# An attention and gated feed-forward block on one core: other lags, durations and placing times in the planner that writes out TensorE's order

## The chip, the cores and the metric

The kernel runs on one core of a Trainium2 chip. The metric is the device time of one execution in microseconds (us), median of three runs. The engines are named as in the profile: PE is TensorE (matmuls, with PEld for its weight loads), DVE is VectorE, ACT is ScalarE, POOL is GpSimd and SP is SyncE, which issues most of the DMAs. PSUM is the memory into which PE writes; each of its eight banks holds 128 rows of 512 float32 values.

## The reference

Two sequences of 1024 tokens with 512 features are normalised. A causal attention with 32 heads of 16 features and a linear position bias (ALiBi) runs on them, and beside it a gated feed-forward net whose weights are reduced to three values and combined by the octonion table. The result is `x + attention * silu(feed-forward)`.

```python
def block(x):
    xn = layernorm(x)                                  # 2 x 1024 x 512
    q, k, v = split(xn @ w_qkv.T + b_qkv)              # 32 heads of 16
    scores = q @ k.T / 4 + slope[head] * position      # causal: later keys get -1e9
    s = softmax(scores) @ v @ w_out.T + b_out
    gate, up = oct(xn, ternary(w_gate)), oct(xn, ternary(w_up))
    g = silu(oct(silu(gate) * up, ternary(w_down)))
    return x + s * g
```

## The kernel before

Attention is cut into 32 units: (batch, group of four heads, half of the queries). A unit is named here as batch/group/half, so 1/0/1 is batch 1, group 0, second half. A unit of half 0 sees 512 keys, one of half 1 sees 1024; they are called first-half and second-half units below.

A unit is worked through in these steps, and every PE step has a matching step on another engine:

- Maxima. PE multiplies queries and keys (L537) into one of two PSUM banks ("x" banks), DVE adds the causal mask on the diagonal blocks and reduces each row to its maximum (`left`, `mx`). `split_max` splits the maxima into two parts on DVE.
- Placing (`place_max`). PE transposes the maxima (L602, tile `pm`), ACT copies them to `mr`, and POOL issues two small DMAs that write `mr` into two rows of the query tile (`q_stack<-mr`). The next product then subtracts the maximum by itself.
- Exponentials. PE multiplies keys and queries again, with the maxima in them (L653), into one of three banks ("e" banks), adds the causal mask by a bf16 matmul on diagonal blocks (L670), and ACT writes `exp` into the tile `p`. The first of these matmuls in a unit waits for the placing DMAs.
- Values. PE multiplies `p` with the values (L689, tile `po`), four matmuls side by side on different columns of the array. `normalise` copies the sum (ACT), transposes it (PE, L709), divides (DVE) and stores it (SP).

Between these, PE also has "side" work that feeds later units or uses finished ones: the projections of queries and keys (L466, `pqk`) and of values (L424, `pv`), the transposes of tokens and weights (L390, L360) and the output projection (L742, L758). These share two "m" banks with the placing and the normalising. Projected queries and keys go through DRAM (`sp<-st`) and come back by SP's DMAs into rings of four query and five key tiles (`k_stack<-sp`, `q_stack<-sp`).

The order in which all of this is issued is not written as loops. A planner in the kernel's Python code (L1046 to the end of `step`) keeps a model clock `now` for PE, and `act` and `dve` for two other engines, in nanoseconds. In each step it has a list of things that could come next, each with the time `ready` at which its banks and inputs are free by the model and with a rank; it takes one, emits its instructions, and moves the clocks. `step` stays with score products (L537, L653) while one is ready within `SOON = 80` of now, and otherwise takes other work that is ready. `SWITCH` is the model's cost of a change between four kinds of matmul: R (scores), V (values), B (bf16 masks), F (all others). The emitted order of PE, ACT, DVE, POOL and SP is kept as it is during the attention.

The model's numbers are therefore what decides the order, and they cost nothing themselves on the chip. The ones in question:

- an ACT or DVE step starts 150 after its matmul has been issued, and its bank is free again 60 after the step's end;
- an exponential takes 510 on ACT, other PSUM copies on ACT take 500, a normalising 600 on DVE;
- `placed[u]`, the time from which the first exponential product of unit `u` may be issued, is 3500 after the model's free time of the placing bank, which is the end of the ACT copy.

After the attention, the feed-forward net runs in an order of plain loops (L1387 and L1421). Its preparation (the splitting of tokens, the expansion of weights) is not held to that order and is moved up by the scheduler into the last units of the attention.

## Time and profile before

| | us |
|---|---|
| median of three runs | 1151.21 (1150.77 to 1151.92) |
| profiled execution, its own time | 1150.65 |
| span of the profiled execution | 1148.9 |
| start: loads, first norms and projections | 0 to 50.0 |
| units of attention, from the first L537 to the last L689 | 50.0 to 849.1 |
| last output projections, then feed-forward net | 849.1 to 1148.9 |

Over the units' stretch of 799.1 us, PE is busy for 746.3 us, DVE for 592.4, ACT for 402.7 and POOL for 71.9, and the mean granted clock of PE is 0.98. A busy PE is not a PE at its peak: a matmul's end is modelled, and lies some 0.16 us behind the point at which the next one may start. PE's useful work is therefore counted below from the spacing of matmuls that follow each other without a wait.

The wait of an engine is put down to the instruction that released it. Idle time on an engine that does not set the end costs nothing by itself.

### The profile page before, as it was taken

What the parts mean: (1) busy time and instruction counts of PE and PEld (TensorE: products, weight loads), DVE (VectorE), ACT (ScalarE), POOL (GpSimd) and SP (SyncE); (2) the same over time, 40 slices, a digit from 0 to 9 for tenths busy, and PEclk for the clock granted to TensorE, in tenths of its full rate; (3) what the DMA queues carried; (4) which work ended last, traced back from release to release, by engine and by line L of the source; (5) the groups of instructions that cost most, each with busy time, mean ns of one, the idle gap of its engine ahead of it and who ended that gap; (6) DMA issues with size and microseconds to landing.
All of it is one profiled execution on the core that took longest, in us unless ns stands there. A gap on an engine that the chain in (4) does not pass through costs nothing.

```text
span 1148.9 us, 15597 instructions
## 1 busy us (share of the span) xinstructions
PE 1067.9 (93%) x5562; PEld 680.9 (59%) x5562; DVE 679.0 (59%) x1400; ACT 500.9 (44%) x962; POOL 176.8 (15%) x295
## 2 busy tenths in 40 slices
PE   7979979999999999989999999899889999999996
PEld 5644545664555665545565555555446687878784
DVE  5368787667777687767787768777641123141211
ACT  4122656645554544535435444465582122232222
POOL 6401023100011010010110000001001123242322
PEclk9899979999999999989999999999899999999998
DMA  6975563453744608082542542831041013030200
GB/s 194 206 147 142 112 169 85 69 87 90 140 112 88 127 2 158 2 195 38 140 66 52 102 90 85 142 62 52 25 140 68 29 45 110 1 110 1 76 35 37
DMA packets 73740, 104.24 MB, mean 91 GB/s; under 512 B 26992, under 2 KB 31120, under 8 KB 73664
## 3 DMA queue, kind: packets, MB, share of 16 engines
q1 hardware_dynamic: 66336, 87.48, 34.8%
q10 hardware_dynamic: 3552, 9.78, 2.7%
q0 software_dynamic: 3776, 5.98, 2.1%
q8 instruction: 45, 0.74, 0.3%
q14 instruction: 31, 0.25, 0.1%
HBM read 69.58 MB, written 33.10 MB: 89 GB/s over the span
## 4 chain that ended last, share of the span: by engine, by line
PE 67%; DVE 12%; DMA 9%; ACT 5%; issue 5%; POOL 2%; SPq 1%; ACTq 0%; DVEq 0%; POOLq 0%
PE s L537 11%; PE s L653 11%; PE po L689 11%; PE pqk L466 6%; PE pg L1387 6%; PE pu L1387 6%; PE pd L1421 5%; DVE mx L69 5%; PE pout L758 4%; DMA q_stack<-mr 3%; PE pv L424 3%; DVE s L69 2%; PE s L670 2%; DVE left L69 1%; ACT p L69 1%
## 5 line engine op out<-in xcount | busy, mean ns | idle before, releaser
L69 ACT ACTIVATE p<-s 128x512 f32<-128x512 f32 x576 | 302.3, 599 | 222.7 <-PE s L670 142.0
L537 PE MATMUL s<-k_stack,q_stack 126*128 126x512 f32 (+3 forms) x768 | 276.3, 417 | 28.2 <-DVE mx L69 22.4
L653 PE MATMUL s<-q_stack,k_stack 128*128 128x512 f32 (+3 forms) x768 | 221.5, 373 | 17.3 <-DMA q_stack<-mr 12.9
L69 DVE TENSOR_REDUCE mx<-s 128x1 f32<-128x384 f32 (+3 forms) x352 | 226.2, 643 | 11.7
L69 DVE TENSOR_REDUCE left<-s 128x1 f32<-128x512 f32 x256 | 169.0, 686 | 86.2 <-PE s L537 85.2
L537 PEld LDWEIGHTS s<-k_stack,q_stack 126*128 126x128 f32 x768 | 133.1, 193 | 128.6 <-issue 33.3
L653 PEld LDWEIGHTS s<-q_stack,k_stack 128*128 128x128 f32 x768 | 135.2, 192 | 74.4 <-ACT p L69 30.2
L69 DVE TENSOR_TENSOR s<-s,mask 128x128 f32<-128x128 f32 (+2 forms) x352 | 124.2, 353 | 62.2 <-PE s L537 61.1
L689 PE MATMUL po<-p,v 128*32 128x512 f32 (+3 forms) x1536 | 143.0, 491 | 0.1
L466 PE MATMUL pqk<-xnT,wq 128*128 128x512 f32 x256 | 131.3, 614 | 4.5 <-POOL wq L69 2.2
L69 DVE SCALAR_TENSOR_TENSOR h<-pu,sc_u,sg 128x512 f32<-128x512 f32 (+1 forms) x44 | 33.1, 751 | 166.1 <-PE pu L1387 158.7
L69 POOL DMA_DIRECT2D q_stack<-mr x64 | 32.0, 505 | 583.6 <-ACT mr L69 583.6
L689 PEld LDWEIGHTS po<-p,v 128*32 128x32 f32 x1536 | 43.4, 109 | 78.8 <-issue 67.3
L69 POOL TENSOR_TENSOR hs<-h,hs 128x512 fp32r<-128x512 f32 (+1 forms) x44 | 57.6, 1309 | 190.1 <-ACT hs L69 190.1
L69 ACT ACTIVATE sg<-pg,sc_g 128x512 f32<-128x512 f32 (+1 forms) x44 | 30.2, 687 | 100.2 <-PE pg L1387 95.3
L424 PE MATMUL pv<-wv,xnT 128*128 128x256 f32 x256 | 68.2, 383 | 1.5 <-DVE v L69 1.5
L758 PE MATMUL pout<-wo_sb,oT 128*128 128x512 f32 x128 | 61.1, 597 | 2.0 <-ACT oT L69 1.0
L466 PEld LDWEIGHTS pqk<-xnT,wq 128*128 128x128 f32 x256 | 47.1, 198 | 26.6 <-issue 18.1
L69 ACT CAST hs<-h 128x512 fp32r<-128x512 f32 (+1 forms) x44 | 27.3, 620 | 75.3 <-DVE h L69 75.3
L670 PE MATMUL s<-mask,ident 128*128 128x256 bf16 (+1 forms) x320 | 52.0, 257 | 0.0
L424 PEld LDWEIGHTS pv<-wv,xnT 128*128 128x128 f32 x256 | 45.8, 190 | 9.8 <-issue 3.2
L69 ACT CAST mr<-pm 8x512 fp32r<-8x512 f32 x32 | 18.3, 572 | 70.7 <-PE pm L602 67.2
(142 smaller groups left out, 1081.1 us busy)
## 6 DMA issues: line engine op xcount, KB each, us to landing
sp<-st SPq DMA_DIRECT2D x32, 512.0 KB
k_stack<-sp SPq DMA_DIRECT2D x128, 128.0 KB
q_stack<-sp SPq DMA_DIRECT2D x128, 128.0 KB
wqr<-in_wqk_dram ACTq DMA_DIRECT2D x16, 512.0 KB
xt<-in_x_dram SPq DMA_DIRECT2D x16, 256.0 KB
att<-o SPq DMA_DIRECT2D x32, 128.0 KB
ot<-att SPq DMA_DIRECT2D x16, 256.0 KB
proj<-y SPq DMA_DIRECT2D x16, 256.0 KB
```

What stands on the lines that cost most here:

```text
L69: ins = issue(*args, **kwargs)
L424: nc.tensor.matmul(ps[:, 0:256], lhsT=xnT[:, c, b * S + kt * P : b * S + (kt + 1) * P], rhs=wv_tiles[2 * b + hh][:, c, :], start=(c == 0), ...
L466: nc.tensor.matmul(ps, lhsT=wq_tiles[b, gp][:, kt, which, :], rhs=xnT[:, kt, b * S + c * 512 : b * S + (c + 1) * 512], start=(kt == 0), st ...
L537: nc.tensor.matmul(ps[:, j * n : (j + 1) * n], lhsT=q_of(b, g, qc)[0 : NR - 2, first + j, tl * P : (tl + 1) * P], rhs=k_of(b, g, c)[0 : NR ...
L653: nc.tensor.matmul(ps[:, c0 : c0 + w], lhsT=k_of(b, g, kt // 4)[0:NR, h, kt % 4 * P : (kt % 4 + 1) * P], rhs=q[0:NR, h, 512 - w : 512], st ...
L670: pe(nc.tensor.matmul(out, lhsT=ident16, rhs=rhs, start=False, stop=True))
L689: nc.tensor.matmul(po[32 * i : 32 * i + 32, 512 - w : 512], lhsT=v[:, kt, h * VC : h * VC + 32], rhs=p[:, i * part + c0 : i * part + c0 + ...
L758: nc.tensor.matmul(ps, lhsT=turned[t][:, c, :], rhs=wo_sb[0][:, c, :], start=(c == 0), stop=(c == KD - 1),)
L1387: nc.tensor.matmul(ps[:fs, :], lhsT=fw[mt][:, n0 + kt, 0:fs], rhs=part[:, kt, :], start=(kt == 0 and n == 0), stop=(kt == KD - 1 and n == 1),)
L1421: nc.tensor.matmul(pd, lhsT=hs[k][:fs, n, st * P : (st + 1) * P], rhs=fw[mt][:fs, 8:12, :].rearrange("p s n -> p (s n)"), start=(mt == 0 a ...
```

## The change

Only the planner's numbers change. `START` and `END` are new names for the lag before a step of ACT or DVE and the lag behind it. Every instruction stays, in number and in form; what changes is the order in which they are emitted, on each engine.

```diff
     SOON = 80
+    START, END = 210, 160
     RUN = 1800
...
             end = run_dve(
-                now[0] + 150,
+                now[0] + START,
                 heads_in * cost * 1.04 + 70 + (heads_in * 135 + 70) * diagonal,
             )
-            take(x_free)[0] = end + 60
+            take(x_free)[0] = end + END
             if n == count - 1:
                 split_max(*units[u], mtiles[u])
-                turns.append((u, run_dve(end, 500) + 100))
+                turns.append((u, run_dve(end, 500) + END))
...
-            end = run_act(now[0] + 150, 510)
-            e_free[e_free.index(HELD)] = end + 60
+            end = run_act(now[0] + START, 485)
+            e_free[e_free.index(HELD)] = end + END
             if i == (3 if len(pieces) == 1 or pieces[0][3] == 384 else 2):
-                p_ready[cells_at[u] + n] = end + 60
+                p_ready[cells_at[u] + n] = end + END
...
                 place_max(*units[u], mtiles[u])
                 run_pe("F", ready, 436)
-                take(m_free)[0] = run_act(now[0] + 150, 500)
-                placed[u] = m_free[0] + 3500
+                take(m_free)[0] = run_act(now[0] + START, 480) + END
+                placed[u] = m_free[0] + 6000
...
                 normalise(*units[u])
                 run_pe("F", t2, 436)
-                take(m_free)[0] = run_dve(now[0] + 150, 600)
+                take(m_free)[0] = run_dve(now[0] + START, 500) + END
...
             if n == last:
-                o_free[0] = run_act(now[0] + 200, 500)
-                norms.append((u, o_free[0] + 100))
+                o_free[0] = run_act(now[0] + START, 480) + END
+                norms.append((u, o_free[0]))
...
             if what == "v":
-                end = run_dve(now[0] + 150, 350)
+                end = run_dve(now[0] + START, 350)
             elif what == "qk":
-                end = run_dve(run_act(now[0] + 150, 600), 700)
+                end = run_dve(run_act(now[0] + START, 600), 700)
...
             elif what == "t":
-                end = run_act(now[0] + 150, 500)
+                end = run_act(now[0] + START, 480)
             else:
-                end = run_dve(now[0] + 150, 600)
-            m_free[m_free.index(HELD)] = end + 60
+                end = run_dve(now[0] + START, 600)
+            m_free[m_free.index(HELD)] = end + END
...
             if what == "t":
-                take(m_free)[0] = run_act(now[0] + 150, 500)
+                take(m_free)[0] = run_act(now[0] + START, 480) + END
```

## The prediction

> **What bounds the kernel now.** I read the page, then the waits, then each unit's stretch (from its first exponential product, L653, to the next unit's).

> The slices show PE nearly full everywhere and DVE at seven tenths until the feed-forward net; ACT has room. The waits say what PE's gaps end on.

> ```profile
> PE   7979979999999999989999999899889999999996
> DVE  5368787667777687767787768777641123141211
> ACT  4122656645554544535435444465582122232222
> ```

> ```profile
> PE s L537 <- DVE mx L69: 22.4, 55, 3.3
> PE s L653 <- DMA q_stack<-mr: 12.9, 7, 3.6
> PE s L653 <- ACT p L69: 3.4, 6, 1.3
> ```

> Two waits lead: maxima that wait for DVE to free an x bank (55 times), and first exponentials that wait for the placing DMA (7 times, up to 3.6 us). PEld loses another 10.6 us to the same DMA. The timeline of PE before unit 1/0/1 shows the worst:

> ```profile
> 498.16 0.60 PE L602 MATMUL pm<-ident,rm 128*8 128x128 f32 x4
> ...
> 503.13 0.41 PE L537 MATMUL s<-k_stack,q_stack 126*128 126x384 f32 x1 [0.24 <-DVE mx L69]
> 507.11 1.62 PE L653 MATMUL s<-q_stack,k_stack 128*128 128x512 f32 x3 [3.56 <-DMA q_stack<-mr]
> ```

> The transposes of the maxima end at 498.6, the DMA lands at 507.0, and PE had 4.2 us of work for these 8.4 us. The third view gives the engines' busy time by stretch (PE, PEld, DVE, ACT, POOL, then the granted clock):

> ```profile
> 342.70:366.70 24.00, 21.89 (x127) 13.14 (x126) 19.80 (x44) 8.91 (x16) 3.05 (x3) 1.00 0.30 73
> 366.70:389.00 22.30, 22.09 (x141) 13.06 (x142) 14.48 (x30) 14.36 (x28) 1.00 (x2) 1.00 0.75 144
> 389.00:410.70 21.70, 20.91 (x132) 15.03 (x130) 18.66 (x44) 6.63 (x13) 2.92 (x10) 1.00 0.46 69
> 722.00:743.70 21.70, 18.84 (x112) 11.29 (x111) 18.86 (x43) 7.71 (x15) 1.00 (x2) 1.00 0.96 164
> ```

> Rows one, three and four are first-half units: DVE works 18.7 to 19.8 us of 21.7 to 24.0, most of it on maxima of later units. The second row, a second-half unit, gives it only 14.5 of 22.3. So PE bounds the attention on average, and in first-half stretches DVE stands just behind it.

> **PE's work.** From spacing without waits: 0.43 us per pass of a 512-wide float32 matmul (two passes each), 0.43 for a 256-wide one in both passes, 0.11 for a transpose, 0.24 for a 512-wide score, 0.06 to 0.11 for a mask, 1.8 for eight 512-wide value matmuls in two rounds of four. Summed over either order this is 648.7 us before and 649.1 after, of the 799.4 us that the stretches take. Some 150 us are waits, changes of kind and slow clock; only these can move.

> **Part 1, `placed` at 6000.** For each unit I summed PE's work between its L602 and its first L653 in both orders, and set the measured time from L602 to the DMA's landing against it. Work before, work after, landing, in us: 0/0/0 3.96, 7.26, 8.17; 0/1/1 2.19, 3.22, 3.62; 0/2/1 3.77, 6.44, 5.82; 0/3/1 4.24, 7.46, 5.24; 0/4/1 3.38, 6.81, 4.55; 0/5/1 4.25, 6.63, 6.42; 1/0/1 4.24, 7.46, 8.38; 1/1/1 4.25, 6.63, 6.58; 1/5/1 3.83, 6.20, 6.62; 1/7/1 1.24, 4.92, 3.45; and the one that gets worse, 1/6/1, 4.16, 2.60, 4.09. Everywhere else the work is longer than the landing. The shortfall, landing less work where positive, is 23.5 us before and 4.1 after: 19.4 us less.

> **What is late next: DVE.** The work moved ahead of those first exponentials is to a good part maxima, and it moves into first-half stretches. I priced DVE's maxima from its rows (0.61 us a step for `left`, 0.85 to 1.38 for mask and `mx` by shape) and took the change in each stretch to its measured busy time. In 342.7:366.7 PE's work goes from 19.3 to 21.0 us and DVE's from 19.8 to 23.5; in 480.3:507.1 PE's from 19.3 to 23.4 and DVE's from 19.5 to 23.0; in 768.1:786.4 PE's from 15.5 to 16.7 and DVE's from 15.1 to 19.6.

> Each of the 33 stretches is then the longer of two sums: PE's work + 2.7 us + its shortfall, or DVE's busy time + an idle rest. The 2.7 is what stretches without a shortfall show over their work (21.7 for 19.0, 24.5 for 21.9, 25.5 for 22.8). DVE's idle rest has no row of its own, as DVE alone binds hardly anywhere now: it is at most the 2.8 us of 722.0:743.7, the least seen, and at least nothing. With 2.8 the sum over all stretches falls by 1.1 us, with nothing by 12.3, with 2.2 by 5.1 (774.4 to 769.3). I take 2.2, nearer the row. So the 19.4 us shrink to **-5.1**, with -12.3 and -1.1 as ends.

> **Part 2, lags 210 and 160, exps 485.** The new lags put 0.86 us between an e bank's matmul and its next use; the trace shows 0.21 from issue to an idle ACT's start, 0.60 for the exp and 0.05 to the next matmul, the same 0.86. Nearest reuse: banks used again with less work between than they need are short by 14.3 us in sum before and 14.1 after for e, 36.7 and 33.9 for x: -3.0. Longer chains get denser: over five tiles in a row the shortfall grows from 12.8 to 19.4 (e) and from 63.5 to 73.2 (x); these windows overlap fourfold, so +4.1. I take the middle, **+0.6**, with -3.0 and +4.1 as ends.

> **Part 3, changes of kind.** PE changes between R, F, V and B 767 times in the old order and 827 in the new; R to F and back grow by 27 each. The stretch 457.0:480.3 has 3.0 us over its work for some 24 changes, so one costs at most 0.125 us: 60 cost 0 to 7.5. About half lie under waits for banks or DVE: **+3.6**.

> **Part 4, the clock.**

> ```profile
> 78.60:82.00 3.40, 3.35 (x10) 2.48 (x11) 1.38 (x2) 0.71 (x2) 0.00 (x0) 0.50 0.04 11
> 505.30:512.10 6.80, 4.99 (x10) 3.32 (x11) 1.01 (x3) 2.83 (x5) 0.00 (x0) 0.50 0.88 180
> 812.50:822.70 10.20, 8.49 (x24) 5.90 (x24) 9.08 (x23) 3.34 (x6) 1.00 (x2) 0.50 0.06 16
> ```

> The clock is granted at 0.50 in five spells; two of them follow PE's waits of 3.3 and 3.8 us for the placing DMA (0/0/0 and 1/0/1). Half of the time in which PE ran in them is lost: 3.4/2 + 5.0/2 = 4.2 us. In the new order these waits fall to 0.9 us each, so **-4.2** (ends -4.2 and 0). The spell at 812.5 follows a DVE step of the feed-forward preparation and stays.

> [...]

> Nothing moves in the feed-forward net, which follows the last unit. POOL and SP issue the same DMAs in nearly the same order, and their landings are taken as they were.

> **Sum.** 1150.65 (own time of the profiled execution, 1.75 over its span) -5.1 +0.6 +3.6 -4.2 = 1145.6. The median lies 0.6 over the profiled execution, so I forecast **1146**. Its own range is 1138 (DVE's rest near nothing) to 1148.8.

> **Rivals.** Only a difference of over 0.2%, 2.3 us, can be told from no change here.

> *Given back, no change (0.18).* DVE's rest is 2.8, one spell stays: -1.1 +0.6 +3.6 -2.5 = +0.6, so 1152. For it: DVE is at 86% in row three already, where the placing never waited. Against: x banks are reused less tightly.

> *DVE takes the place of the placing, slower (0.36).* PE issues the moved maxima in a bunch into two x banks, waits for DVE inside first-half stretches, and exponentials find less other work between them in the second-half ones. With 3.0 us of rest Part 1 gains nothing, with 4.0 it costs 4.2; then +4.2 +0.6 +3.6 and no clock gained is +8.4, so 1160. It decides from a rest of 3.0. For it: in six first-half stretches (0/2/0 to 0/5/0, 1/0/0, 1/1/0) DVE now rests over 4 us. Against: in most of these PE waits for the placing meanwhile.

> *The placing lands later too (0.06 of the 0.36).* The late landings (over 5 us) fall together with the fills of key and query tiles. If these meet the DMA again and the shortfall stays at 23.5, the stretches' sum grows by 6.3 instead: +10.5 with the two other parts, 1162. Against: the work is 6.2 to 7.5 us, and most landings took 3.3 to 4.

> **Chances and range.** Faster 0.46, within 0.2% 0.18, slower 0.36. The ends reach from all gains (-12.3, -3.0, 0, -4.2: 1131) to 1162; 1135 to 1160 leaves one in ten on each side.

> **What would show it.** Right: PE's waits on `q_stack<-mr` fall from 12.9 to under 4 us, and no half clock at 78 and 505. DVE is at over 90% in the stretches of 0/5/0, 1/0/0 and 1/6/0, and `mx` waits grow. Wrong: waits on the placing as long as before, or PE's waits on `mx` above 35 us, or first-half stretches longer by over 2 us each without shorter second-half ones.

## The result, and the profile after

The changed kernel takes 1158.25 us (median of five runs, 1155.54 to 1159.65) against 1151.92 (1150.77 to 1152.98) for the kernel before: a ratio of 1.0054, 95% interval 1.0038 to 1.007. It is slower by half a per cent, where 1146 was forecast. The profiled execution is the fastest of the five: 1155.54, span 1153.8, 4.9 over that of the kernel before. The attention's units take 802.9 us of it (50.4 to 853.3) against 799.1; start and end add 0.4 and 0.7.

The slices of the page and PE's waits after (line and tile, the releaser; us in total, times, longest):

```profile
PE   7889979999999999699999999899889999999996
DVE  4386786767768677577787777778642123141211
ACT  4122646654653543436436455364682122232321
PEclk9899979999999999799999999998899999999998
```

```profile
PE s L537 <- DVE mx L69: 31.1, 37, 11.4
PE s L653 <- ACT p L69: 8.0, 10, 1.6
PE s L653 <- DMA q_stack<-mr: 0.4, 1, 0.4
```

The wait for the placing is gone, 12.9 us to 0.4, as the change meant it. The maxima wait fewer times (37 for 55) but longer, and one of these waits alone is 11.4 us. It lies in the one dent of PE's row (slice 17), where the granted clock dips too. PE's timeline there, at the first exponentials of unit 0/7/1:

```profile
460.45 0.70 PE L653 MATMUL s<-q_stack,k_stack 128*128 128x512 f32 x2 [0.45 <-DMA q_stack<-mr]
472.61 0.77 PE L537 MATMUL s<-k_stack,q_stack 126*128 126x512 f32 x1 [11.45 <-DVE mx L69]
```

Two exponentials are issued, then nothing for 11.45 us. DVE is named, but DVE was itself waiting for ACT:

```profile
470.91 0.75 DVE L69 SCALAR_TENSOR_TENSOR st<-pqk,bqk_sb,st 128x512 fp32r<-128x512 f32 x1 [11.46 <-ACT st L69]
```

ACT's timeline (ACTq is its instruction that starts a DMA):

```profile
448.11 0.69 ACT L69 ACTIVATE st<-pqk,bqk_sb 128x512 fp32r<-128x512 f32 x1 [0.17 <-PE pqk L466]
...
455.18 0.69 ACT L69 ACTIVATE st<-pqk,bqk_sb 128x512 fp32r<-128x512 f32 x1 [0.29 <-PE pqk L466]
455.32 0.82 ACTq L69 DMA_DIRECT2D wqr<-in_wqk_dram  x2
470.19 0.69 ACT L69 ACTIVATE st<-pqk,bqk_sb 128x512 fp32r<-128x512 f32 x1 [14.32 <-DMA sp<-st]
```

ACT stands for 14.3 us before writing a third projected tile. `st` has two buffers, so the third has to wait until the first, written at 448.1, has been stored (`sp<-st`). Why that store was late stands in SP's timeline:

```profile
434.47 1.71 SPq L69 DMA_DIRECT2D q_stack<-sp  x4
459.25 2.17 SPq L69 DMA_DIRECT2D k_stack<-sp  x4
461.47 0.28 SPq L69 DMA_DIRECT2D k_stack<-al_dram  x1
461.85 0.39 SPq L69 DMA_DIRECT2D att<-o  x1
462.33 1.84 SPq L69 DMA_DIRECT2D q_stack<-sp  x4
464.39 0.38 SPq L69 DMA_DIRECT2D sp<-st  x1
```

SP issues nothing from 436 to 459, and the store comes fifth behind a fill of a key tile for unit 1/0. What the fill waited for is in the waits of SP:

```profile
SPq L69 <- DMA wqr<-in_wqk_dram: 34.9, 4, 23.1
```

That is a load of projection weights. The fill neither reads nor overwrites them. What links the two stands in the DMAs' records in the traces: in both kernels SP's and ACT's DMAs signal on the same eight semaphores, 101 and 104 to 110. The load issued at 455.32 signals on 101, last at 459.24; the first DMA of the fill waits for 101 and is issued at 459.25.

```
ACT   455.32  wqr <- weights in DRAM         signals on 101
SP    459.25  key fill <- sp, first of four  waits for 101, signals on 101
```

So SP stands until a load has landed that ACT issues only at 455.32. It is a chain of four steps between two engines: ACT issues the weights late; SP's fill waits for them; the store behind the fill is late; ACT needs that store's buffer. ACT keeps its emitted order, so the exponentials stand behind that `st` (the next comes at 470.8), DVE's half of `st` too, then the x banks, then PE.

The stretch of 0/7/1 shows the price (PE, PEld, DVE, ACT, POOL busy, granted clock, DMA share, GB/s); first before, then after:

```profile
457.00:480.30 23.30, 22.96 (x133) 12.60 (x132) 16.61 (x32) 14.12 (x27) 1.00 (x2) 1.00 0.08 26
```

```profile
345.50:370.00 24.50, 23.80 (x137) 15.66 (x134) 20.55 (x48) 7.76 (x14) 1.03 (x2) 1.00 0.68 141
460.50:493.90 33.40, 21.46 (x126) 12.17 (x127) 16.28 (x32) 14.21 (x27) 2.92 (x10) 0.80 0.52 119
493.90:519.60 25.70, 25.07 (x133) 13.89 (x131) 21.17 (x47) 9.46 (x17) 0.99 (x2) 1.00 0.59 114
770.60:794.90 24.30, 21.63 (x120) 12.54 (x119) 19.91 (x42) 7.94 (x15) 2.88 (x3) 0.90 0.27 56
```

Unit 0/7/1 takes 33.4 us where it took 23.3, and PE's work in it, counted as in the prediction, is 17.5 where it was 20.3: 12.9 us are lost in this one stretch, more than the units lost in all (3.8). All other units together are then faster than before.

The other rows are the three first-half stretches in which DVE was forecast at over 90%. It is at 84% (20.55 of 24.50), 82% and 82%. Only the last, 1/6/0, got longer as feared: 24.3 us for 18.3. There PE issues nothing but maxima from 786 to 795, in step with DVE.

The clock, in the stretches at half speed that are new:

```profile
281.20:284.70 3.50, 3.50 (x17) 1.62 (x19) 2.04 (x3) 3.50 (x7) 0.08 (x1) 0.51 0.59 238
462.10:475.80 13.70, 3.19 (x8) 2.38 (x9) 4.43 (x10) 3.34 (x6) 0.00 (x0) 0.50 0.91 226
745.50:748.90 3.40, 3.40 (x9) 2.53 (x10) 0.99 (x2) 2.02 (x4) 0.00 (x0) 0.50 0.40 140
789.80:800.10 10.30, 9.29 (x21) 6.43 (x22) 8.63 (x18) 3.78 (x7) 0.00 (x0) 0.50 0.00 0
```

The spells at 78 and 505 went, as forecast, but these came, and one of 3.4 us at 90: 54.6 us at half clock in the units for 34.1. Two of them lie in the jam and in the run of maxima of 1/6/0. (The columns are those of the stretches.)

### The profile page after: what moved, and what is told of

Read it like the earlier page. It is cut to its first block, busy times and chain, and to the rows that moved or that the text cites. A ratio compares the mean times of both kernels' runs of the same rounds, so it can differ in the third digit from the quotient of the medians.

```text
span 1153.8 us, 15593 instructions
## 1 busy us (share of the span) xinstructions
PE 1069.0 (93%) x5562; PEld 682.2 (59%) x5562; DVE 677.9 (59%) x1400; ACT 500.8 (43%) x962; POOL 177.0 (15%) x295
## 3 DMA queue, kind: packets, MB, share of 16 engines
q1 hardware_dynamic: 66336, 87.48, 34.5%
## 4 chain that ended last, share of the span: by engine, by line
PE 72%; DVE 12%; issue 5%; DMA 5%; ACT 4%; POOL 2%; SPq 0%; ACTq 0%; DVEq 0%; POOLq 0%
PE s L537 12%; PE s L653 12%; PE po L689 11%; PE pqk L466 7%; PE pg L1388 6%; PE pu L1388 6%; PE pd L1422 5%; DVE mx L69 5%; PE pout L758 4%; PE pv L424 3%; DVE s L69 2%; PE s L670 2%; PE pm L602 1%; DMA ot<-att 1%; ACT p L69 1%
## 5 line engine op out<-in xcount | busy, mean ns | idle before, releaser
L69 ACT ACTIVATE p<-s 128x512 f32<-128x512 f32 x576 | 303.3, 600 | 184.4 <-PE s L670 125.0
L537 PE MATMUL s<-k_stack,q_stack 126*128 126x512 f32 (+3 forms) x768 | 278.4, 421 | 38.0 <-DVE mx L69 31.1
L653 PE MATMUL s<-q_stack,k_stack 128*128 128x512 f32 (+3 forms) x768 | 225.3, 379 | 8.6 <-ACT p L69 8.0
L69 DVE TENSOR_REDUCE mx<-s 128x1 f32<-128x384 f32 (+3 forms) x352 | 226.3, 643 | 11.8
L537 PEld LDWEIGHTS s<-k_stack,q_stack 126*128 126x128 f32 x768 | 133.7, 195 | 149.7 <-issue 51.7
L69 DVE TENSOR_REDUCE left<-s 128x1 f32<-128x512 f32 x256 | 168.7, 685 | 83.2 <-PE s L537 81.8
L653 PEld LDWEIGHTS s<-q_stack,k_stack 128*128 128x128 f32 x768 | 136.0, 194 | 60.4 <-ACT p L69 26.2
L69 DVE TENSOR_TENSOR s<-s,mask 128x128 f32<-128x128 f32 (+2 forms) x352 | 124.1, 353 | 60.8 <-PE s L537 59.7
L69 DVE SCALAR_TENSOR_TENSOR h<-pu,sc_u,sg 128x512 f32<-128x512 f32 (+1 forms) x44 | 33.0, 751 | 166.3 <-PE pu L1388 158.7
L69 POOL DMA_DIRECT2D q_stack<-mr x64 | 32.4, 511 | 622.2 <-ACT mr L69 622.2
L69 POOL TENSOR_TENSOR hs<-h,hs 128x512 fp32r<-128x512 f32 (+1 forms) x44 | 57.5, 1307 | 190.2 <-ACT hs L69 190.2
L69 ACT ACTIVATE sg<-pg,sc_g 128x512 f32<-128x512 f32 (+1 forms) x44 | 30.2, 687 | 100.9 <-PE pg L1388 95.5
L69 ACT ACTIVATE st<-pqk,bqk_sb 128x512 fp32r<-128x512 f32 x32 | 22.0, 689 | 113.6 <-PE pqk L466 71.8
L69 ACT CAST hs<-h 128x512 fp32r<-128x512 f32 (+1 forms) x44 | 27.3, 620 | 75.2 <-DVE h L69 75.2
```

Source lines behind the costliest of these rows:

```text
L69: ins = issue(*args, **kwargs)
L537: nc.tensor.matmul(ps[:, j * n : (j + 1) * n], lhsT=q_of(b, g, qc)[0 : NR - 2, first + j, tl * P : (tl + 1) * P], rhs=k_of(b, g, c)[0 : NR ...
L653: nc.tensor.matmul(ps[:, c0 : c0 + w], lhsT=k_of(b, g, kt // 4)[0:NR, h, kt % 4 * P : (kt % 4 + 1) * P], rhs=q[0:NR, h, 512 - w : 512], st ...
```

## Experiments

Two theories at first. *The link*: the loss is the jam in 0/7/1, and comes from a store and a fill behind a late load on another engine's queue. *The order*: the new order is worse by itself (DVE in the place of the placing, changes of kind), and the jam is one of its faces. Two edits cut the link in different places, and each was also made to the kernel before as control. In the diffs, `act_`, `sp_` and `pool_` are the engines that issue.

**Loads of wqr issued by POOL.** ACT then issues only the first of these loads, at the start, and the orders of PE, DVE and SP stay as they are. In the changed kernel, and in the kernel before:

```diff
-                load_wq((n // NP, n % NP), act_)
+                load_wq((n // NP, n % NP), pool_)
```

> The changed kernel with one edit: the loads of the query and key weights (wqr) are issued by POOL and not by ACT; the orders of PE, DVE and SP stay as they are. Theory (a jam on SP's queue): in the changed kernel the fill of a key tile stands on SP behind a completion count that it shares with a wqr load, which ACT issues only at 455.3; the store of a projection (sp<-st) stands behind that fill, ACT's next st waits 14.3 us for the store, and PE idles 11.4 us and then runs at half clock. With the load off ACT the fill no longer waits for it: the wait of ACT st on sp<-st goes, the stretch 460 to 494 falls from 33.4 us to 20 to 22, and the kernel takes 1143 to 1148 us. Rival (VectorE has taken the place of the placing): the jam is hidden behind DVE's work or returns elsewhere; 1154 to 1159 us.

> The kernel before with the same edit, as a control. Theory: the old order has no projection store that anybody waits for behind such a fill (ACT never waits for sp<-st there), so the edit is worth little: 1147 to 1153 us; a part of the late placings may go if they came from fills that start late. Rival (the edit itself is what gains, in any order): it falls by as much as in the changed kernel, 8 us or more.

Measured: the changed kernel 1143.89 us, ratio to before 0.9932 [0.9908, 0.9956]; the control 1145.29, 0.9945 [0.9926, 0.9963]. In the first, SP waits for no wqr any more, ACT waits for no `sp<-st`, and 0/7/1 takes 22.7 us. The jam is gone, and the changed kernel has lost its handicap. But the kernel before gains as well, more than its bounds allowed, which was worth learning; with this edit the two kernels can't be told apart. Some of its late placings had the same root: 1/0/0 shrinks from 26.8 to 22.5 us, and half of PE's wait on the placing goes (12.9 before), as its waits show:

```profile
PE s L537 <- DVE mx L69: 24.3, 61, 3.5
PE s L653 <- DMA q_stack<-mr: 6.8, 4, 3.4
```

**The store `sp<-st` issued by POOL.** The link between the load and the fill stays; the store no longer stands behind the fill. The orders of PE, DVE and ACT stay.

```diff
-            sp_.dma_start(
+            pool_.dma_start(
                 out=parts[b, gp][which][:, :, c * 512 : (c + 1) * 512].rearrange(
```

> The changed kernel with another link of the chain taken out: the stores of the projections (sp<-st) are issued by POOL, so that they no longer stand behind the fills on SP; wqr stays on ACT, and PE's order is the same. Theory: SP's fill still waits for wqr, but ACT's st no longer waits for the store; the 11.4 us stall goes and the kernel takes 1143 to 1150 us. Rival (the fill itself is late and PE waits for it, whatever the stores do): 1154 us or more.

> The kernel before with the projection stores (sp<-st) on POOL, the control to the changed kernel with the same edit (1140.7 us). Theory: in the old order no st waits for a store, so the stores' queue matters little, and the late placing landings stay, since SP's fills still wait for wqr: 1146 to 1152 us; the net worth of the new plan's order without the jam is then 5 to 11 us. Rival (the new order is worth nothing): 1139 to 1143 us.

Measured: 1140.69, ratio 0.9907 [0.9888, 0.9925]; the kernel before with the same edit 1153.75, 1.0017 [1.0001, 1.0033]. In the first, SP waits for wqr longer than ever and nobody minds:

```profile
SPq L69 <- DMA wqr<-in_wqk_dram: 138.5, 11, 29.6
```

```profile
462.40:484.20 21.80, 20.75 (x126) 11.09 (x127) 15.41 (x32) 13.64 (x26) 3.72 (x11) 1.00 0.59 133
```

The second row is the stretch of 0/7/1, at full clock. So SP's 138.5 us of waits go with the shortest time so far; what cost 12.9 us in 0/7/1 of the changed kernel was a store behind such a wait. The kernel before had 84.5 us of such waits, and a store stood behind the longest of them too:

```profile
SPq L69 <- DMA wqr<-in_wqk_dram: 84.5, 8, 34.5
```

```profile
459.50 0.69 ACT L69 ACTIVATE st<-pqk,bqk_sb 128x512 fp32r<-128x512 f32 x1
...
488.64 0.70 ACT L69 ACTIVATE st<-pqk,bqk_sb 128x512 fp32r<-128x512 f32 x1
...
491.03 0.37 SPq L69 DMA_DIRECT2D sp<-st  x1
```

The tile written at 459.5 was stored only at 491.0, yet ACT never waited: the next `st`, at 488.6, had the other buffer, and the one after it came at 499.7. So a late store is not enough for a jam; a third tile must be due before it has gone out. In the new order it was due at 455.9. With this edit the new order is 13.1 us faster than the old; the control lies 1.8 over its upper bound.

**One part alone, queues as they were.** `placed` at 6000 in the kernel before, and the lags and durations without it (the changed kernel with 3500):

```diff
-                placed[u] = m_free[0] + 3500
+                placed[u] = m_free[0] + 6000
```

> The kernel before with the placing time alone changed, 3500 to 6000. Theory: this is the part that gains; the waits of the first exponentials on the placing DMA fall from 12.9 us on PE to under 3, and the time to 1138 to 1146 us, unless the new order meets a jam on SP by chance, which would show as a wait of ACT st on sp<-st. Rival (VectorE takes the place): 1150 to 1156 us with the waits on mx above 30 us and no jam.

> The changed kernel with the placing back at 3500 and nothing else: the lags and durations alone, with the loads of wqr on ACT and the stores on SP as in both kernels. Theory (the new lags gain some 8 us by themselves, 1153.75 to 1145.24 with the stores on POOL; the jam in 0/7/1 comes from how the fills, a store and a late load of wqr stand to one another): without a jam 1143 to 1147, with one of 14 us in any stretch 1150 to 1155, and the trace then shows ACT waiting for sp<-st. Rival (the gain of the lags hangs on the stores having left SP): 1150 or more with no wait of ACT on sp<-st.

Measured: the placing alone 1151.84, 1.0005 [0.9989, 1.0021], with PE's waits on it down to 2.6 us; the lags alone 1155.80, 1.0045 [1.0028, 1.0062]. The jam in 0/7/1 comes with the lags: the second kernel has one too, in the same unit, which takes 36.8 us (its time is 0.8 over the bounds for a jam). SP's and ACT's timelines there:

```profile
440.86 2.28 SPq L69 DMA_DIRECT2D k_stack<-sp  x4
464.12 0.23 SPq L69 DMA_DIRECT2D k_stack<-al_dram  x1
```

```profile
460.63 0.34 ACTq L69 DMA_DIRECT2D wqr<-in_wqk_dram  x1
460.99 0.61 ACT L69 ACTIVATE p<-s 128x512 f32<-128x512 f32 x1
461.00 0.44 ACTq L69 DMA_DIRECT2D wqr<-in_wqk_dram  x1
474.79 0.69 ACT L69 ACTIVATE st<-pqk,bqk_sb 128x512 fp32r<-128x512 f32 x1 [13.20 <-DMA sp<-st]
```

This time it is the fill's fifth DMA, the position row, that stands from 443 to 464 behind the load of 460.6 (21.0 us, SP's longest wait for wqr there).

The placing alone also makes ACT wait for a store, once and for half as long, near the start of the attention:

```profile
79.21 0.69 ACT L69 ACTIVATE st<-pqk,bqk_sb 128x512 fp32r<-128x512 f32 x1 [6.92 <-DMA sp<-st]
```

No wait of SP for wqr stands before it, and the first exponential comes at 79.0 where it came at 78.6 before, so it is not the jam of 0/7/1. The time of the placing alone lies in the rival's range, but the rival's sign is missing: PE's waits on `mx` are 17.1 us, not over 30. Where the time goes that PE no longer waits for the placing isn't shown.

**The parts, with the store on POOL.** Lags alone, placing alone, and the placing half way, at 4500, with the new lags:

> The changed kernel with the stores on POOL and the placing time put back to 3500: the new lags and durations alone. If the gain of the plan is in the placing time, the waits on q_stack<-mr return (10 us or more on PE and PEld) and it takes 1146 to 1152 us. Rival (the gain is in the lags): 1138 to 1143 us.

> The kernel before with the stores on POOL and the placing time alone at 6000. If the gain is in the placing time: 1138 to 1144 us. Rival (the gain needs the lags as well, or lies in them): 1146 to 1152 us.

> The changed kernel with the stores on POOL and a placing time of 4500. In the changed kernel's stretch 770.6 to 794.9 nothing but maxima is left while the placing DMA has landed at 789.8 and its exponential comes at 794.9: 6000 waits for too long there (24.3 us against 18.3 before). Theory (6000 over-waits where side work has run out): 1136 to 1141 us, with most waits on q_stack<-mr still gone. Rival (the late landings of 5 to 8 us decide): those waits return and it takes 1143 to 1150 us.

Measured: 1145.24, 0.9939 [0.992, 0.9957]; 1155.27, 1.003 [1.0017, 1.0042]; 1140.54, 0.99 [0.9882, 0.9917]. The lags give 8.5 us (from 1153.75), the placing alone none (1.5 worse, with intervals that overlap), and the placing on top of the lags 4.6. 4500 and 6000 can't be told apart. Only the run at 4500 lies within bounds set for it: the first time falls between its two ranges, the second 3.3 over the rival's.

**The last corners.** Lags alone with the loads on POOL, and both edits in the new and the old order:

> The changed kernel with the placing at 3500 and the loads of wqr issued by POOL: the fourth corner beside the kernel before (1145.29) and the changed kernel (1143.89) with the same edit. If the lags gain by themselves in whatever queue: 1136 to 1140, and the late placing then costs 4 to 8 us there. If what the lags gain is the same time that the late loads of wqr cost (banks reused while DVE and the placing are late): 1143 to 1146, and nothing is to be had twice. PE's waits on q_stack<-mr: 4 to 8 us, as in the kernel before with that edit (6.8).

> The changed kernel with both the loads of wqr and the projection's stores issued by POOL. If both edits take away one and the same link, nothing is added to the better one: 1139 to 1143. If each has a cost of its own (the store behind a waiting fill; late fills): 1134 to 1138. If POOL, which also issues the placing, is then too full: over 1144, with PE's waits on q_stack<-mr above 3 us.

> The kernel before with both the loads of wqr and the stores issued by POOL, as control to the one with both in the new order. The stores alone gave the old order nothing (1153.75 against 1152.13) and the loads alone 6.3 us (1145.29), so 1144 to 1148; the new order is then 3 to 8 us faster than the old where both are taken off.

Measured: 1142.04, 0.9905 [0.9884, 0.9925]; 1139.80, 0.9898 [0.9877, 0.9919]; 1149.03, 0.9968 [0.9956, 0.9981]. The first falls between its ranges, the second in the range of one and the same link. The last missed its bounds by 1 us, and the new order is 9.2 us faster there, not 3 to 8: with both edits the old order is 3.7 us slower than with the loads alone, and why stays open. The medians in one view:

| us | queues as they were | loads on POOL | stores on POOL | both |
|---|---|---|---|---|
| old lags, 3500 | 1151.92 | 1145.29 | 1153.75 | 1149.03 |
| old lags, 6000 | 1151.84 | | 1155.27 | |
| new lags, 3500 | 1155.80 | 1142.04 | 1145.24 | |
| new lags, 6000 | 1158.25 | 1143.89 | 1140.69 | 1139.80 |

The new lags lose only in the first column, the one with the link whole. Without it they gain 3.3 us or 8.5, and with the placing 1.4 (within the noise), 13.1 and 9.2. Three of these kernels, and the one with 4500, are about 1% under the kernel before; the best, 1139.80, can't be told from 1140.54 or 1140.69.

**Is it the size of the lags, or the luck of one order?** The new kernel with the stores on POOL, its lags alone stepped (new durations, placing at 6000 throughout):

```diff
-    START, END = 210, 160
+    START, END = 190, 140
```

and likewise 230 and 180, 150 and 60 (the old lags), and 170 and 100.

> The changed kernel with the stores on POOL (1140.69 with 210 and 160), its lags at 190 and 140. If the longer lags gain by their size, because banks are reused less tightly, the time lies between, near the changed kernel's: 1140 to 1144. If each order that the planner writes has its own luck, some microseconds up or down: as likely 1144 to 1150 as under it.

> The same with lags of 230 and 180. By the size of the lags: 1138 to 1142, as the change goes a little further in the same direction. By luck of the order: 1144 or more is as likely.

> The same with the old lags, 150 and 60, but the new durations (exps 485, copies 480, normalising 500) and the placing at 6000. If the lags carry the gain: 1152 to 1156, as the old planner with the placing at 6000 (1155.27). If the durations carry it: 1140 to 1145. If the two go together: between.

> The same with lags of 170 and 100, half way. By the size of the lags: 1145 to 1150. By luck of the order: anything from 1140 to 1158, out of line with its neighbours at 150/60 and 190/140.

| lags | 150/60 | 170/100 | 190/140 | 210/160 | 230/180 |
|---|---|---|---|---|---|
| us | 1149.45 | 1150.00 | 1143.35 | 1140.69 | 1153.57 |
| ratio to before | 0.9977 | 0.9984 | 0.9913 | 0.9907 | 1.001 |
| interval | 0.9964 to 0.999 | 0.9973 to 0.9996 | 0.9892 to 0.9934 | 0.9888 to 0.9925 | 0.9997 to 1.0022 |

Up to 210/160 longer lags look better, by 9 us over four points, though not from the first to the second. Then 20 ns more cost 12.9. The old lags with the new durations, 1149.45, lie 5.8 under the old planner with the placing at 6000 (1155.27), so the durations carry a part, or the lag behind the copies and the normalising, where the old planner had none. In the order of 230/180, a wait shows in 1/5/0 (30.5 us for 22.9) that none of the planner's numbers stands for:

```profile
739.21 0.45 PE L537 MATMUL s<-k_stack,q_stack 126*128 126x384 f32 x1
745.49 1.08 PE L742 MATMUL pot<-ident,ot 128*128 128x128 f32 x4 [5.84 <-DMA ot<-att]
```

PE is led to a transposition whose tile is still under way from DRAM. That unit's 7.6 us are the greater part of the 12.9; the rest isn't shown. So both answers have something for them: the size of the lags may do something, and some of the written orders draw single waits of 5.8 to 14.3 us on DMAs.

## Why the prediction was wrong

**The step that failed** is the sentence "POOL and SP issue the same DMAs in nearly the same order, and their landings are taken as they were." The list of DMAs is the same, but SP's waits for ACT's loads of wqr are not: 84.5 us in eight waits before, 34.9 in four after. The fill that mattered was held for 23.1 us, the store behind it held ACT for 14.3, and 0/7/1 lost 12.9 us. With the link cut the changed kernel takes 1140.69 or 1143.89, under the forecast of 1146. The warning was in the profile of before and was not weighed: one of those eight waits lasted 34.5 us, and behind it a store went out 31 us after its tile, with no `st` that needed the buffer.

**Part 1, the placing.** The mechanism was right as to the waits: they fell from 12.9 to 0.4 us, and the landings no longer bind. (PEld did not lose "another" 10.6 us: five of its six waits are the same moments as PE's.) Its worth was mis-sized: -5.1 forecast with ends of -12.3 and -1.1; alone it gives nothing (1151.84; 1155.27 for 1153.75), on top of the new lags 4.6. What was "late next" wasn't DVE in most places. DVE stayed at 82 to 84% where over 90% was forecast; its work in the three stretches, put at 23.5, 23.0 and 19.6 us, measured 20.55, 21.17 and 19.91, so it was put too high in two of them. Without the jam the `mx` waits don't grow (21.4 us with the store moved, 22.4 before). The placing's and the lags' parts were summed as if each stood alone; measured, they don't add, and why the placing is worth nothing alone stays open.

**Part 2, the lags.** Forecast +0.6, ends -3.0 and +4.1. Measured, with the new durations, -8.5 with the store on POOL, -3.3 with the loads there, and +3.9 (1155.80 for 1151.92) with the jam they bring. The two sizes without the jam lie beyond the forecast's lower end, the second only just. Counting tight reuses of banks could not size it, as an order can bring single waits of 6 to 14 us that the count doesn't see.

**Part 3, changes of kind.** There are 60 more, as counted. Their cost wasn't measured alone. The order with the most of them (834, placing at 4500) is among the fastest, which speaks against a large one.

**Part 4, the clock.** Two spells of half clock went, as forecast, for -4.2. But PE was busy for 39.7 us at half clock in the units, for 26.8 before. By the step's own estimate (half of it is lost; in the spell at 78.6 a score follows another after 0.43 us, where the prediction counts 0.24) that is 6.4 us more, where 4.2 less was forecast. The sum had no term for a new spell.

It also let both spells go because PE's waits before them were to fall to 0.9 us. (They are 3.52 and 3.56 us in PE's rows, not 3.3 and 3.8.) That a spell needs a wait that long, no row showed: PE's wait before 1/0/1 lasts from 503.5 to 507.1, and the half clock begins at 505.3, 1.8 us into it. The runs showed less to be enough. Windows of 3.4 us from the run of maxima, one after the other, in the changed kernel:

```profile
783.00:786.40 3.40, 3.40 (x16) 1.92 (x14) 3.23 (x10) 0.01 (x1) 0.00 (x0) 1.00 0.03 8
786.40:789.80 3.40, 1.74 (x7) 0.89 (x6) 3.21 (x7) 0.57 (x1) 0.98 (x2) 1.00 0.64 190
789.80:793.20 3.40, 2.75 (x6) 1.42 (x6) 2.76 (x6) 0.00 (x0) 0.00 (x0) 0.50 0.00 0
793.20:796.60 3.40, 3.04 (x8) 2.27 (x9) 2.96 (x7) 1.07 (x3) 0.00 (x0) 0.50 0.00 0
796.60:800.10 3.50, 3.50 (x10) 2.75 (x9) 2.91 (x6) 2.71 (x6) 0.00 (x0) 0.50 0.00 0
800.10:803.50 3.40, 3.40 (x24) 1.45 (x24) 2.26 (x9) 3.10 (x11) 0.00 (x0) 1.00 0.02 5
```

PE is busy for 1.74 of 3.40 us in the second, in waits of 1.2 us at most, and the three windows after it run at half clock, until one of them is full. In the spell from 820.5 one full window (3.40 of 3.41 us) was not enough for the return.

**The sum.** The two profiled executions differ by +4.9: +12.9 of time lost in 0/7/1, +0.4 of PE's work, +1.1 at both ends, and by difference -9.5 of time lost in all other stretches. These did more than the -5.1 that all four parts were to bring; the jam ate it. The own range's upper end, 1148.8, does not come out of the terms: with -1.1 for the first they give 1149.6.

**The rivals.** None described it. *DVE takes the place of the placing* happened in one stretch, 1/6/0 (+6.0), not in the six named (0/3/0 grew by 4.9, but PE waits there for `mx` for 0.4 us only); its sign, `mx` waits over 35 us, did not come (31.1, 11.4 of it the jam). *The placing lands later too* didn't happen. *Given back, no change* fits the placing alone, but not through DVE. That the time lies near the 1160 of the first and inside the range, 1135 to 1160, is luck: the reason is neither's.

What stays open: why the new order is better by itself where the stores have left SP, stall by stall, and how much of that would outlive the next small edit to the planner.

## What to carry to other kernels

A wait that costs nothing today can be a debt on the queue that holds it: before an order is changed, read every queue's long waits and what stands behind them, and name the buffer that becomes scarce if one of those lands late. Where such a buffer is about to be needed, try loads that aren't urgent and stores that free it on different queues: here 1143.89 us with the loads on POOL and 1140.69 with the stores there, for 1158.25 (in the old order the stores' queue was worth nothing, 1153.75 for 1151.92). And where a planner writes the order, one order's time is one draw: neighbouring settings, here 20 ns apart, show whether a gain is the setting's or the draw's.
